# Attention without row maxima behind a branch on the chip, and the scan's C rows made on TensorE

## The chip, the core and the metric

The kernel runs on one core of a Trainium2 chip. The core has five engines with their own instruction queues: TensorE (PE in the profile, its weight loads are PEld), VectorE (DVE), ScalarE (ACT), GpSimd (POOL) and SyncE (SP, which here only issues transfers). They meet at semaphores. SBUF is the working memory of 128 partitions, PSUM takes the results of TensorE. The metric is the time of one execution in microseconds, as the device measures it; lower is better. All data are 32-bit floats.

## What is computed

Four images of 128 channels and 64x64 pixels pass four layers. Each layer is `x + f(group_norm(x))`, with 32 groups. In `f` stand, one after the other: full attention over the 4096 pixels, a 5x5 convolution, a state-space scan in two directions, and a 3x3 convolution. The two layers that the change touches are these (cut to what matters):

```python
# layer 0, n = 4096 pixels, c = 128 channels
q = einsum('bnc,dc->bnd', xt, Wq) + bq            # k and v likewise
scores = einsum('bic,bjc->bij', q, k) * c ** -0.5
attn = softmax(scores, axis=-1)
out = einsum('bij,bjc->bic', attn, v)

# layer 2, for each half of 64 channels (the second runs backwards in time)
xc = silu(causal_conv4(u)); xt = xc.transpose(0, 2, 1)
delta = softplus(xt @ Wd + bd)
Bm = xt @ WB                                       # 64 states n
Cm = xt @ WC
dA = exp(delta[..., None] * A)
dBx = (delta * xt)[..., None] * Bm[:, :, None, :]
h[t] = dA[t] * h[t-1] + dBx[t]                     # for each channel d and state n
y = einsum('bldn,bln->bld', h, Cm) + Dp * xt
```

## The kernel before

The program is written out without loops on the chip. An image lives in SBUF as 128 channels by 4096 pixels; almost every operation works on a tile of 128 partitions by 1024 columns (`CH`), of which there are four (`NCH`). A matrix product of that size is two instructions of 512 columns, and each of them appears in the profile as two matmul records and two weight loads. PSUM is given out in two pools of two buffers each: `psum_s` for short results and `psum_a` for accumulators. Work tiles come from `w2` (two buffers for each tag) and `w3` (three).

The Python program gives the tasks and the data they need; a scheduler sets the order in each engine's queue, and within a queue instructions run in that order. Each waits on semaphores for its inputs, and for the last reader of the buffer that it overwrites.

**Attention** (`attention`, line 218). After the group norm, `qT` (already scaled) and `kT` are made with channels on partitions, and `v` with pixels on partitions. Queries are taken in four blocks `qb` of 1024. For the softmax the kernel first finds the maximum of every score row: `row_max_piece` (line 245) makes a tile of scores with queries on partitions, `pmax`, on TensorE, and VectorE reduces it to a column (`part`, line 252). There are 32 such pieces for a block. `row_max_spread` (line 254) turns the 1024 maxima into a tile `mb` in which every partition holds them. The pieces of the first block run alone, ahead of the loop (line 268); those of block `qb + 1` are put between the steps of block `qb` (line 282).

The loop over the 32 key tiles `j` makes scores with keys on partitions (`sc`, TensorE), subtracts `mb` (`sm`, line 285, VectorE), takes the exponential (`pt`, line 287, ScalarE), adds it to a running sum (`lsum`, line 292, GpSimd) and multiplies it with the values (`values`, line 276, TensorE, into `acc`), one step behind the scores. At the end of a block a product with a matrix of ones (`pl`) sums `lsum` over partitions, VectorE takes the reciprocal (`rec`, line 299) and multiplies, and GpSimd adds the result to the image (line 302). In the first image the weights of the 5x5 convolution are also built on VectorE in this stretch (`build_conv_weights`).

**Scan** (`scan_layer`, line 345). A stage that I call the preparation makes `xc`, `delta` and `dx = delta * xc`, and the B and C rows of all states: two products, `pB` and `pCm`, are copied to SBUF (`bs`, `cs`) and written to DRAM (`bmat`, `cmat`). Channels of the forward half lie on partitions 0 to 63, those of the backward half on 64 to 127, and `bdiag` holds the weights of both halves on the diagonal.

Then comes the loop of four chunks `c` of 1024 time steps and 64 states `n`, 256 states for each image. For one state: four transfers on SP's queue bring the B row and the C row of each half from DRAM, repeated over its 64 partitions (`bb`, `cc`, line 427); ScalarE makes `da` (line 432); GpSimd makes `db = dx * bb` (line 434); VectorE runs the recurrence `h` (line 436, a scan along the tile) and multiplies by the C row, `hc = cc * h` (line 442); TensorE adds `hc` to `yacc` with an identity matrix as weights (`add_state`), one state behind. ScalarE keeps the last column of `h` for the next chunk (`last`, line 440). `db`, `h`, `da` and `hc` have two buffers each, so `db` of state n + 2 waits until `h` of state n has been computed. At the end of a chunk VectorE takes `yacc` over into `yn` (line 449), and after four chunks a product `po` and a sum close the layer.

These are the lines on which the order in the scan rests:

```python
db = w2.tile([P, CH], F32, tag="w1", name=f"db_{uid}")
nc.gpsimd.tensor_tensor(db, dx[:, cut], bb, ALU.mult)
h = w2.tile([P, CH], F32, tag="w2", name=f"h_{uid}")
nc.vector.tensor_tensor_scan(
    h, da, db, 0.0 if c == 0 else last[n], ALU.mult, ALU.add
)
hc = w2.tile([P, CH], F32, tag="w4", name=f"hc_{uid}")
nc.vector.tensor_tensor(hc, cc, h, ALU.mult)
```

Of the kernel before, what the change touches and what calls it, by code (L numbers as in the profile page):

```python
# [25 lines left out]
P = 128  # L26
# [3 lines left out]
MM = 512  # L30
HALF = P // 2
PAD = 2


BQ, BK, BX, BP, CONVB, BD, DSKIP, MAINB, CONVW, ALOG = 0, 1, 2, 3, 4, 5, 6, 7, 8, 12
# [3 lines left out]
def conv_preact_kernel(  # L39
# [41 lines left out]
    def psum_s(name):  # L81
        return ps_s.tile([P, CH], F32, tag="s", name=name)

    def psum_a(name):
        return ps_a.tile([P, CH], F32, tag="a", name=name)

    def matmul_ch(dst, lhsT, rhs, start=True, stop=True):
        for h in range(CH // MM):
            cut = bass.ts(h, MM)
            nc.tensor.matmul(dst[:, cut], lhsT, rhs[:, cut], start=start, stop=stop)  # L90
# [36 lines left out]
    def col(i):  # L127
        return vec[:, i : i + 1]
# [6 lines left out]
    for d in range(2):  # L135
        r = slice(d * HALF, (d + 1) * HALF)
        nc.gpsimd.tensor_copy(bdiag[r, :, r], ssm_sb[r, :, :])

    a_neg = const.tile([P, NST], F32, name="a_neg")
    nc.scalar.activation(a_neg, vec[:, ALOG : ALOG + NST], AF.Exp)  # L140
# [74 lines left out]
        nc.vector.tensor_scalar(dst, src, gm, rs, ALU.subtract, ALU.mult)  # L215


    def attention(b, xs, after_qkv):
        xn = big.tile([P, L], F32, tag="b0", name=f"xn0_{b}")
        group_norm(xs, xn, f"a{b}")  # L220
        qT = big.tile([P, L], F32, tag="b1", name=f"qT_{b}")
        kT = big.tile([P, L], F32, tag="b2", name=f"kT_{b}")
        v = big.tile([P, NJT, C], F32, tag="b4", name=f"v_{b}")
        for c in range(NCH):
            cut = bass.ts(c, CH)
            pq = psum_s(f"pq_{b}_{c}")
            matmul_ch(pq, wm[:, 0, :], xn[:, cut])
            nc.vector.tensor_scalar(qT[:, cut], pq, col(BQ), scale, ALU.add, ALU.mult)
            pk = psum_s(f"pk_{b}_{c}")
            matmul_ch(pk, wm[:, 1, :], xn[:, cut])  # L230
            nc.scalar.activation(kT[:, cut], pk, AF.Identity, bias=col(BK))
        for c in range(NCH):
            pv = psum_a(f"pv_{b}_{c}").rearrange("p (t c) -> p t c", c=C)
            for t in range(TPB):
                j = c * TPB + t
                nc.tensor.matmul(
                    pv[:, t, :], xn[:, bass.ts(j, P)], wm[:, 2, :], start=True, stop=True
                )
            bvb = bv_b.unsqueeze(1).to_broadcast([P, TPB, C])
            nc.vector.tensor_tensor(v[:, c * TPB : (c + 1) * TPB, :], pv, bvb, ALU.add)  # L240
        after_qkv()

        parts = {}

        def row_max_piece(qb, i):

            t, kc = divmod(i, NCH)
            if i == 0:
                parts[qb] = small.tile([P, TPB, NCH], F32, tag="part", name=f"part_{b}_{qb}")
            pp = psum_s(f"pmax_{b}_{qb}_{i}")  # L250
            matmul_ch(pp, qT[:, qb * CH + t * P : qb * CH + (t + 1) * P], kT[:, bass.ts(kc, CH)])
            nc.vector.tensor_reduce(parts[qb][:, t, kc : kc + 1], pp, AX.X, ALU.max)  # L252

        def row_max_spread(qb):

            m = small.tile([P, TPB], F32, tag="rmax", name=f"rmax_{b}_{qb}")
            nc.vector.tensor_reduce(m, parts.pop(qb), AX.X, ALU.max)
            pb = psum_s(f"pmb_{b}_{qb}")
            for t in range(TPB):
                nc.tensor.matmul(  # L260
                    pb[:, bass.ts(t, P)], m[:, t : t + 1].to_broadcast([P, P]), ident,
                    start=True, stop=True,
                )
            mb = w2.tile([P, CH], F32, tag="w0", name=f"mb_{b}_{qb}")
            nc.scalar.copy(mb, pb)  # L265
            return mb

        for i in range(NJT):
            row_max_piece(0, i)
        for qb in range(NCH):  # L270
            mb = row_max_spread(qb)
            acc = psum_a(f"acc_{b}_{qb}")
            lsum = w2.tile([P, CH], F32, tag="w1", name=f"lsum_{b}_{qb}")
            weights = []

            def values(j):
                matmul_ch(acc, v[:, j, :], weights[j], start=j == 0, stop=j == NJT - 1)

            for j in range(NJT):
                sc = psum_s(f"sc_{b}_{qb}_{j}")  # L280
                matmul_ch(sc, kT[:, bass.ts(j, P)], qT[:, bass.ts(qb, CH)])
                if qb + 1 < NCH:
                    row_max_piece(qb + 1, j)
                sm = w2.tile([P, CH], F32, tag="w2", name=f"sm_{b}_{qb}_{j}")
                nc.vector.tensor_tensor(sm, sc, mb, ALU.subtract)  # L285
                pt = w3.tile([P, CH], F32, tag="w3", name=f"pt_{b}_{qb}_{j}")
                nc.scalar.activation(pt, sm, AF.Exp)  # L287
                weights.append(pt)
                if j == 1:
                    nc.gpsimd.tensor_tensor(lsum, weights[0], pt, ALU.add)  # L290
                elif j > 1:
                    nc.gpsimd.tensor_tensor(lsum, lsum, pt, ALU.add)  # L292
                if j > 0:
                    values(j - 1)
            values(NJT - 1)
            pl = psum_s(f"pl_{b}_{qb}")
            matmul_ch(pl, ones, lsum)
            rec = w2.tile([P, CH], F32, tag="w2", name=f"rec_{b}_{qb}")
            nc.vector.reciprocal(rec, pl)
            nc.vector.tensor_tensor(rec, acc, rec, ALU.mult)  # L300
            cut = bass.ts(qb, CH)
            nc.gpsimd.tensor_tensor(xs[:, cut], xs[:, cut], rec, ALU.add)


    def conv(b, xs, weights, k, bias, name, finished=None):
# [39 lines left out]
    def scan_layer(b, xs):  # L345
# [25 lines left out]
        delta = big.tile([P, L], F32, tag="b3", name=f"delta_{b}")  # L371
        dx = big.tile([P, L], F32, tag="b4", name=f"dx_{b}")
        bmat = dram.tile([P, L], F32, tag="bmat", name=f"bmat_{b}")
        cmat = dram.tile([P, L], F32, tag="cmat", name=f"cmat_{b}")
        for c in range(NCH):
            cut = bass.ts(c, CH)
            pb = psum_s(f"pB_{b}_{c}")
            matmul_ch(pb, bdiag[:, 1, :], xc[:, cut])
            bs = w2.tile([P, CH], F32, tag="w0", name=f"bs_{b}_{c}")
            nc.scalar.copy(bs, pb)  # L380
            nc.sync.dma_start(bmat[:, cut], bs)
            pcm = psum_s(f"pCm_{b}_{c}")
            matmul_ch(pcm, bdiag[:, 2, :], xc[:, cut])
            cs = w2.tile([P, CH], F32, tag="w4", name=f"cs_{b}_{c}")
            nc.vector.tensor_copy(cs, pcm)
            nc.scalar.dma_start(cmat[:, cut], cs)

            pz = psum_s(f"pz_{b}_{c}")  # L390
            matmul_ch(pz, bdiag[:, 0, :], xc[:, cut])
            nc.vector.tensor_scalar(delta[:, cut], pz, col(BD), 0.0, ALU.add, ALU.max)
            e = w2.tile([P, CH], F32, tag="w1", name=f"e_{b}_{c}")
            nc.scalar.activation(e, pz, AF.Abs, bias=col(BD))
            nc.scalar.activation(e, e, AF.Exp, scale=-1.0)
            u1 = w2.tile([P, CH], F32, tag="w2", name=f"u1_{b}_{c}")
# [10 lines left out]
        c_dnt = cmat.rearrange("(d n) t -> d n t", d=2)  # L407
# [4 lines left out]
        for c in range(NCH):  # L412
# [7 lines left out]
            for n in range(NST):  # L420
                uid = f"{b}_{c}_{n}"

                bb = w3.tile([P, CH], F32, tag="w3", name=f"bb_{uid}")
                cc = w3.tile([P, CH], F32, tag="cc", name=f"cc_{uid}")
                for to, of_dnt in ((bb, b_dnt), (cc, c_dnt)):
                    for d in range(2):
                        nc.sync.dma_start(
                            to[d * HALF : (d + 1) * HALF, :],
                            of_dnt[d, n : n + 1, cut].to_broadcast([HALF, CH]),
                        )  # L430
# [11 lines left out]
                nc.vector.tensor_tensor(hc, cc, h, ALU.mult)  # L442
                held.append(hc)
                if n > 0:
                    add_state(n - 1)
# [85 lines left out]
```

## Time and profile before

| | |
|---|---|
| time, median of 3 runs | 10353.79 us (10353.5 to 10355.77) |
| profiled execution, its own time | 10353.79 us |
| profiled execution, span from first to last instruction | 10352.1 us |
| mean granted TensorE clock | 0.769 of full speed |
| PE busy | 7380.1 us (71%) |
| DVE busy | 7715.1 us (75%) |
| ACT busy | 1958.2 us (19%) |
| POOL busy | 3692.0 us (36%) |
| moved by DMA | 1113.78 MB |

The four images follow one another with hardly any overlap, so the span shows the same picture four times. The page cuts the span into 40 slices, ten for an image; a digit is the busy share in tenths, PEclk the granted clock:

```profile
PE   8998555556999855555699975555569997555556
DVE  6542999998454299999845439999975533999997
POOL 2450444443245044444224404444422441444442
PEclk9999666666999966666799986666679998666667
DMA  0000777775000077777500017777750001777774
```

Each row of ten reads from left to right: about four slices of attention and the 5x5 convolution, then about six of scan, the 3x3 convolution at their edge. A sum over the whole span mixes these stages, whose limits differ; what an operation costs has to be read in its own stage.

### The profile page before, as it was taken

The page shows a single profiled execution, that of the slowest core. Times are in us where ns is not written, and L with a number is a line of the kernel's source. Part 1 is how long each engine was busy: PE and PEld are TensorE (multiplying, and loading weights), DVE is VectorE, ACT ScalarE, POOL GpSimd, SP SyncE. Part 2 cuts the span into 40 slices and gives each one's busy share as a digit, 9 for nine tenths or more (in the row PEclk, how much of TensorE's full clock was granted, in tenths as well). Part 3 has the DMA queues.
Part 4 walks back from the last instruction along what each step waited for, and adds up shares of the span by engine and source line. Part 5 has one row for each costly group of instructions (what it writes and reads, how often), then busy time and mean ns, then how long its engine had stood idle before and what let it go on. Part 6 is the DMA issues. An engine that isn't in the chain of part 4 may idle for free. (4 is left out here: it accounts for less than half of the span.)

```text
span 10352.1 us, 46831 instructions
## 1 busy us (share of the span) xinstructions
PE 7380.1 (71%) x13504; PEld 2812.2 (27%) x13504; DVE 7715.1 (75%) x3693; ACT 1958.2 (19%) x2458; POOL 3692.0 (36%) x1618
## 2 busy tenths in 40 slices
PE   8998555556999855555699975555569997555556
PEld 3443111112444311111244431111124443111112
DVE  6542999998454299999845439999975533999997
ACT  1121222221122122222112212222111221222211
POOL 2450444443245044444224404444422441444442
PEclk9999666666999966666799986666679998666667
DMA  0000777775000077777500017777750001777774
GB/s 29 0 0 25 176 179 178 182 178 139 15 0 0 29 181 178 178 182 178 133 13 0 0 36 182 180 178 182 178 126 2 0 0 45 184 179 179 182 178 117
DMA packets 337445, 1113.78 MB, mean 108 GB/s; under 512 B 66976, under 2 KB 67616, under 8 KB 336672
## 3 DMA queue, kind: packets, MB, share of 16 engines
q1 hardware_dynamic: 334160, 1101.26, 42.3%
q10 hardware_dynamic: 3024, 9.51, 0.2%
q8 instruction: 106, 1.74, 0.1%
q14 instruction: 155, 1.27, 0.0%
HBM read 1085.34 MB, written 25.17 MB: 107 GB/s over the span
## 5 line engine op out<-in xcount | busy, mean ns | idle before, releaser
L90 PE MATMUL yacc<-hc,ident 128*128 128x512 f32 x4096 | 3414.5, 981 | 2620.4 <-DVE hc L442 2620.4
L434 POOL TENSOR_TENSOR db<-dx,bb 128x1024 f32<-128x1024 f32 x1024 | 2436.3, 2379 | 3492.0 <-DVE h L436 3489.7
L442 DVE TENSOR_TENSOR hc<-cc,h 128x1024 f32<-128x1024 f32 x1024 | 3408.8, 3329 | 93.8 <-issue 3.6
L90 PEld LDWEIGHTS yacc<-hc,ident 128*128 128x128 f32 x4096 | 1050.8, 283 | 4984.1 <-DVE hc L442 4036.7
L436 DVE TENSOR_TENSOR_SCAN h<-da,last,db 128x1024 f32<-128x1024 f32 x768 | 1846.5, 2404 | 0.4
L292 POOL TENSOR_TENSOR lsum<-lsum,pt 128x1024 f32<-128x1024 f32 x480 | 1125.8, 2345 | 1128.8 <-ACT pt L287 1128.8
L285 DVE TENSOR_TENSOR sm<-sc,mb 128x1024 f32<-128x1024 f32 x512 | 626.1, 1223 | 1083.1 <-PE sc L90 1082.9
L432 ACT ACTIVATE da<-delta,a_neg 128x1024 f32<-128x1024 f32 x1024 | 1172.7, 1145 | 1170.0 <-DVE h L436 1169.8
L90 PE MATMUL pmax<-kT,qT 128*128 128x512 f32 x2048 | 951.9, 596 | 41.6 <-DVE part L252 26.5
L90 PE MATMUL sc<-qT,kT 128*128 128x512 f32 x2048 | 964.3, 593 | 20.6 <-ACT mb L265 13.2
L90 PE MATMUL acc<-pt,v 128*128 128x512 f32 x2048 | 962.1, 592 | 3.3 <-ACT pt L287 3.3
L287 ACT ACTIVATE pt<-sm 128x1024 f32<-128x1024 f32 x512 | 541.0, 1057 | 1867.2 <-DVE sm L285 1864.5
L440 ACT COPY last<-h 128x1 f32<-128x1 f32 x768 | 146.9, 191 | 3534.3 <-DVE h L436 3534.3
L252 DVE TENSOR_REDUCE part<-pmax 128x1 f32<-128x1024 f32 x512 | 626.5, 1224 | 211.7 <-PE pmax L90 211.5
L320 PE MATMUL pce<-xpe,cw 128*128 128x512 f32 x1600 | 699.5, 599 | 13.3 <-DVE xpe L215 13.3
L436 DVE TENSOR_TENSOR_SCAN h<-da,db 128x1024 f32<-128x1024 f32 x256 | 609.0, 2379 | 19.2 <-POOL db L434 19.2
L90 PEld LDWEIGHTS pmax<-kT,qT 128*128 128x128 f32 x2048 | 387.8, 190 | 540.8 <-issue 424.4
L90 PEld LDWEIGHTS sc<-qT,kT 128*128 128x128 f32 x2048 | 387.7, 190 | 507.3 <-issue 476.8
L90 PEld LDWEIGHTS acc<-pt,v 128*128 128x128 f32 x2048 | 388.8, 190 | 494.4 <-issue 484.5
L329 DVE TENSOR_TENSOR x<-pce,x 128x1024 f32<-128x1024 f32 x16 | 19.6, 1225 | 669.3 <-PE pce L320 669.3
L320 PEld LDWEIGHTS pce<-xpe,cw 128*128 128x128 f32 x1600 | 304.0, 190 | 405.9 <-issue 392.2
L320 PE MATMUL pcm<-xpm,m 128*128 128x512 f32 x576 | 258.2, 609 | 13.3 <-DVE xpm L215 13.3
(143 smaller groups left out, 1639.6 us busy)
## 6 DMA issues: line engine op xcount, KB each, us to landing
cc<-cmat SPq DMA_DIRECT2D x2048, 256.0 KB, 4.1
bb<-bmat SPq DMA_DIRECT2D x2048, 256.0 KB, 4.9
bmat<-bs SPq DMA_DIRECT2D x16, 512.0 KB, 3.0
cmat<-cs ACTq DMA_DIRECT2D x16, 512.0 KB, 2.6
out_dram<-x SPq DMA_DIRECT2D x16, 512.0 KB, 2.6
x<-in_x_dram SPq DMA_DIRECT2D x3, 2048.0 KB, 8.2
x<-in_x_dram SPq DMA_DIRECT2D x4, 512.0 KB, 6.5
xx_sb<-in_xhat_dram SPq DMA_DIRECT2D x1, 1600.0 KB, 13.5
```

Of the source, the lines that this page charges most:

```text
L90: nc.tensor.matmul(dst[:, cut], lhsT, rhs[:, cut], start=start, stop=stop)
L252: nc.vector.tensor_reduce(parts[qb][:, t, kc : kc + 1], pp, AX.X, ALU.max)
L285: nc.vector.tensor_tensor(sm, sc, mb, ALU.subtract)
L287: nc.scalar.activation(pt, sm, AF.Exp)
L292: nc.gpsimd.tensor_tensor(lsum, lsum, pt, ALU.add)
L320: nc.tensor.matmul(acc[:, bass.ts(h, MM)].rearrange("p (r w) -> p r w", w=W), weights[:, t, :], xp[:, y : y + rows, dx : dx + W], start=t ...
L329: nc.vector.tensor_tensor(xs[:, cut], acc, xs[:, cut], ALU.add)
L432: nc.scalar.activation(da, delta[:, cut], AF.Exp, scale=a_neg[:, n : n + 1])
L434: nc.gpsimd.tensor_tensor(db, dx[:, cut], bb, ALU.mult)
L436: nc.vector.tensor_tensor_scan(h, da, db, 0.0 if c == 0 else last[n], ALU.mult, ALU.add)
L440: nc.scalar.copy(last[n], h[:, CH - 1 : CH])
L442: nc.vector.tensor_tensor(hc, cc, h, ALU.mult)
```

## The change

Three things change.

- **Attention gets a second form.** After `qT`, `kT` and `v`, the largest squared norm of the queries and of the keys is found: the tiles are squared on ScalarE, summed over channels with the matrix of ones on TensorE (`pn`), and reduced on VectorE. The product of the two bounds the square of every score. If it is at most 1600 (`SAFE_SCORE` squared), the exponentials can't overflow and no maximum need be subtracted. Every engine loads the outcome into a register and branches. One arm, `softmax_plain`, takes the exponential straight from the scores in PSUM; the other, `softmax_shifted`, is the old form. Both are in the program, one after the other.
- **The C rows are no longer stored.** `pCm`, `cs` and `cmat` go. For each state ScalarE copies the state's column of C weights, repeated 64 times for each half, into a 128x128 tile `wsel`; a product of `wsel` with `xc` gives the C row on all partitions in PSUM (`pc`, in the profile `pC`), and `hc` reads it there.
- **The B row comes in one transfer** over all 128 partitions in place of two over 64.

The old form of attention stays as it was, under a new name. The diff, cut to its core (moved lines left out):

```diff
+SAFE_SCORE = 40.0
...
+    wc_dn = bdiag[:, 2, :].rearrange("p (d n) -> p d n", d=2)
...
+    def softmax_plain(b, xs, qT, kT, v):
+
+        for qb in range(NCH):
+            cut = bass.ts(qb, CH)
+            acc = psum_a(f"facc_{b}_{qb}")
+            lsum = w2.tile([P, CH], F32, tag="w1", name=f"flsum_{b}_{qb}")
+            weights = []
+
+            def values(j):
+                matmul_ch(acc, v[:, j, :], weights[j], start=j == 0, stop=j == NJT - 1)
+
+            for j in range(NJT):
+                sc = psum_s(f"fsc_{b}_{qb}_{j}")
+                matmul_ch(sc, kT[:, bass.ts(j, P)], qT[:, cut])
+                pt = w3.tile([P, CH], F32, tag="w3", name=f"fpt_{b}_{qb}_{j}")
+                nc.scalar.activation(pt, sc, AF.Exp)
+                weights.append(pt)
+                if j == 1:
+                    nc.gpsimd.tensor_tensor(lsum, weights[0], pt, ALU.add)
+                elif j > 1:
+                    nc.gpsimd.tensor_tensor(lsum, lsum, pt, ALU.add)
+                if j > 0:
+                    values(j - 1)
+            values(NJT - 1)
+            pl = psum_s(f"fpl_{b}_{qb}")
+            matmul_ch(pl, ones, lsum)
+            rec = w2.tile([P, CH], F32, tag="w2", name=f"frec_{b}_{qb}")
+            nc.vector.reciprocal(rec, pl)
+            nc.vector.tensor_tensor(rec, acc, rec, ALU.mult)
+            nc.gpsimd.tensor_tensor(xs[:, cut], xs[:, cut], rec, ALU.add)
+
+    def softmax_shifted(b, xs, qT, kT, v):
...
+        most = small.tile([P, 2, NCH], F32, tag="most", name=f"most_{b}")
+        for i, src in enumerate((qT, kT)):
+            for c in range(NCH):
+                sq = w2.tile([P, CH], F32, tag="w2", name=f"sq_{b}_{i}_{c}")
+                nc.scalar.activation(sq, src[:, bass.ts(c, CH)], AF.Square)
+                pn = psum_s(f"pn_{b}_{i}_{c}")
+                matmul_ch(pn, ones, sq)
+                nc.vector.tensor_reduce(most[:, i, c : c + 1], pn, AX.X, ALU.max)
+        both = small.tile([P, 2], F32, tag="both", name=f"both_{b}")
+        nc.vector.tensor_reduce(both, most, AX.X, ALU.max)
+        prod = small.tile([P, 1], F32, tag="prod", name=f"prod_{b}")
+        nc.vector.tensor_tensor(prod, both[:, 0:1], both[:, 1:2], ALU.mult)
+        small_i = small.tile([P, 1], I32, tag="small_i", name=f"small_i_{b}")
+        nc.vector.tensor_scalar(small_i, prod, SAFE_SCORE * SAFE_SCORE, None, ALU.is_le)
+        is_small = nc.values_load(small_i[0:1, 0:1], min_val=0, max_val=1)
+        with tc.If(is_small > 0) as small_scores:
+            softmax_plain(b, xs, qT, kT, v)
+        with small_scores.Else():
+            softmax_shifted(b, xs, qT, kT, v)
...
-        cmat = dram.tile([P, L], F32, tag="cmat", name=f"cmat_{b}")
...
-            pcm = psum_s(f"pCm_{b}_{c}")
-            matmul_ch(pcm, bdiag[:, 2, :], xc[:, cut])
-            cs = w2.tile([P, CH], F32, tag="w4", name=f"cs_{b}_{c}")
-            nc.vector.tensor_copy(cs, pcm)
-            nc.scalar.dma_start(cmat[:, cut], cs)
...
-                cc = w3.tile([P, CH], F32, tag="cc", name=f"cc_{uid}")
-                for to, of_dnt in ((bb, b_dnt), (cc, c_dnt)):
-                    for d in range(2):
-                        nc.sync.dma_start(
-                            to[d * HALF : (d + 1) * HALF, :],
-                            of_dnt[d, n : n + 1, cut].to_broadcast([HALF, CH]),
-                        )
+                nc.sync.dma_start(bb, b_dnt[:, n : n + 1, cut].to_broadcast([2, HALF, CH]))
+                wsel = w3.tile([P, 2, HALF], F32, tag="wsel", name=f"wsel_{uid}")
+                nc.scalar.copy(wsel, wc_dn[:, :, n : n + 1].to_broadcast([P, 2, HALF]))
+                pc = psum_s(f"pC_{uid}")
+                matmul_ch(pc, wsel.rearrange("p d e -> p (d e)"), xc[:, cut])
+
...
-                nc.vector.tensor_tensor(hc, cc, h, ALU.mult)
+                nc.vector.tensor_tensor(hc, pc, h, ALU.mult)
```

More of the change, by code (lines that the diff above doesn't have):

```diff
@@ L215, in group_norm @@
         nc.vector.tensor_scalar(dst, src, gm, rs, ALU.subtract, ALU.mult)
[L218 to L237, printed above, removed]
-                )
-            bvb = bv_b.unsqueeze(1).to_broadcast([P, TPB, C])
-            nc.vector.tensor_tensor(v[:, c * TPB : (c + 1) * TPB, :], pv, bvb, ALU.add)
-        after_qkv()
@@ L302, in attention @@
             nc.gpsimd.tensor_tensor(xs[:, cut], xs[:, cut], rec, ALU.add)
+    def attention(b, xs, after_qkv):
+        xn = big.tile([P, L], F32, tag="b0", name=f"xn0_{b}")
+        group_norm(xs, xn, f"a{b}")
+        qT = big.tile([P, L], F32, tag="b1", name=f"qT_{b}")
+        kT = big.tile([P, L], F32, tag="b2", name=f"kT_{b}")
+        v = big.tile([P, NJT, C], F32, tag="b4", name=f"v_{b}")
+        for c in range(NCH):
+            cut = bass.ts(c, CH)
+            pq = psum_s(f"pq_{b}_{c}")
+            matmul_ch(pq, wm[:, 0, :], xn[:, cut])
+            nc.vector.tensor_scalar(qT[:, cut], pq, col(BQ), scale, ALU.add, ALU.mult)
+            pk = psum_s(f"pk_{b}_{c}")
+            matmul_ch(pk, wm[:, 1, :], xn[:, cut])
+            nc.scalar.activation(kT[:, cut], pk, AF.Identity, bias=col(BK))
+        for c in range(NCH):
+            pv = psum_a(f"pv_{b}_{c}").rearrange("p (t c) -> p t c", c=C)
+            for t in range(TPB):
+                j = c * TPB + t
+                nc.tensor.matmul(
+                    pv[:, t, :], xn[:, bass.ts(j, P)], wm[:, 2, :], start=True, stop=True
+                )
+            bvb = bv_b.unsqueeze(1).to_broadcast([P, TPB, C])
+            nc.vector.tensor_tensor(v[:, c * TPB : (c + 1) * TPB, :], pv, bvb, ALU.add)
+        after_qkv()
+        most = small.tile([P, 2, NCH], F32, tag="most", name=f"most_{b}")
+        for i, src in enumerate((qT, kT)):
+            for c in range(NCH):
+                sq = w2.tile([P, CH], F32, tag="w2", name=f"sq_{b}_{i}_{c}")
[14 more added lines that the diff above has]
+            softmax_shifted(b, xs, qT, kT, v)
@@ L406, in scan_layer @@
         b_dnt = bmat.rearrange("(d n) t -> d n t", d=2)
-        c_dnt = cmat.rearrange("(d n) t -> d n t", d=2)
         last = [
@@ L423, in scan_layer @@
                 bb = w3.tile([P, CH], F32, tag="w3", name=f"bb_{uid}")
-                cc = w3.tile([P, CH], F32, tag="cc", name=f"cc_{uid}")
-                for to, of_dnt in ((bb, b_dnt), (cc, c_dnt)):
-                    for d in range(2):
-                        nc.sync.dma_start(
-                            to[d * HALF : (d + 1) * HALF, :],
-                            of_dnt[d, n : n + 1, cut].to_broadcast([HALF, CH]),
-                        )
+                nc.sync.dma_start(bb, b_dnt[:, n : n + 1, cut].to_broadcast([2, HALF, CH]))
[3 more added lines that the diff above has]
+                matmul_ch(pc, wsel.rearrange("p d e -> p (d e)"), xc[:, cut])
                 da = w2.tile([P, CH], F32, tag="w0", name=f"da_{uid}")
```

## The prediction

> **What bounds the kernel now.** I read three views in this order: the table of stages, the costliest groups, then the timeline of single engines inside the two long stages. The table of stages, for the first image (attention, 5x5 convolution, preparation of the scan, scan, 3x3 convolution; columns: stretch, its length, busy time of PE, weight load, DVE, ACT and POOL, then TensorE clock, DMA share, GB/s):
>
> ```profile
> 137.50:784.00 646.50, 620.27 (x1477) 276.21 (x1476) 312.99 (x249) 139.31 (x132) 301.50 (x133) 0.99 0.00 0
> 784.00:967.00 183.00, 175.87 (x404) 76.98 (x404) 13.58 (x19) 0.00 (x0) 0.65 (x2) 0.98 0.00 0
> 967.00:1046.00 79.00, 37.59 (x64) 14.12 (x64) 58.14 (x49) 34.41 (x31) 12.01 (x9) 0.74 0.29 93
> 1046.00:2538.50 1492.50, 853.98 (x1024) 262.86 (x1024) 1456.93 (x520) 311.00 (x447) 607.15 (x256) 0.63 0.72 178
> ```
>
> Attention is bound by PE (620 of 646 us), the scan by DVE (1457 of 1492). The scan's DVE rows do not fit together, as the groups show:
>
> ```profile
> L442 DVE TENSOR_TENSOR hc<-cc,h 128x1024 f32<-128x1024 f32 x1024 | 3408.8, 3329 | 93.8 <-issue 3.6
> L285 DVE TENSOR_TENSOR sm<-sc,mb 128x1024 f32<-128x1024 f32 x512 | 626.1, 1223 | 1083.1 <-PE sc L90 1082.9
> L299 DVE RECIPROCAL rec<-pl 128x1024 f32<-128x1024 f32 x16 | 104.9, 6557 | 70.4 <-PE pl L90 70.4
> ```
>
> The same operation on the same shape takes 3329 ns as `hc` (both inputs in SBUF) and 1223 ns as `sm` (one input in PSUM). DVE and POOL side by side, first in the usual rhythm of the scan:
>
> ```profile
> 1499.03 2.34 DVE L436 TENSOR_TENSOR_SCAN h<-da,last,db 128x1024 f32<-128x1024 f32 x1
> 1501.45 2.34 POOL L434 TENSOR_TENSOR db<-dx,bb 128x1024 f32<-128x1024 f32 x1 [3.42 <-DVE h L436]
> 1501.46 3.42 DVE L442 TENSOR_TENSOR hc<-cc,h 128x1024 f32<-128x1024 f32 x1
> 1504.80 2.34 DVE L436 TENSOR_TENSOR_SCAN h<-da,last,db 128x1024 f32<-128x1024 f32 x1
> ```
>
> A scan releases the `db` after next; `db` starts 10 ns ahead of `hc`, and `hc` lasts 3.42 = 2.34 + 1.08: it stands still until `db` ends. Scans start 5.77 apart. At the start of a chunk the turns are swapped:
>
> ```profile
> 1426.56 1.23 DVE L442 TENSOR_TENSOR hc<-cc,h 128x1024 f32<-128x1024 f32 x1
> 1426.60 3.38 POOL L434 TENSOR_TENSOR db<-dx,bb 128x1024 f32<-128x1024 f32 x1 [2.23 <-DVE h L436]
> 1427.70 4.43 DVE L436 TENSOR_TENSOR_SCAN h<-da,last,db 128x1024 f32<-128x1024 f32 x1
> ```
>
> Here `hc` runs freely, `db` is held, and the scan is held by `db` in turn: it ends at 1432.13, 2.15 after `db` (1429.98). In attention the two engines overlap and neither suffers:
>
> ```profile
> 8394.00 2.35 POOL L292 TENSOR_TENSOR lsum<-lsum,pt 128x1024 f32<-128x1024 f32 x1 [1.02 <-ACT pt L287]
> 8394.98 1.22 DVE L285 TENSOR_TENSOR sm<-sc,mb 128x1024 f32<-128x1024 f32 x1 [2.21 <-PE sc L90]
> ```
>
> [...]matmul records stand 0.43 us apart in dense work and 0.86 in much of the scan, whose clock is 0.63.[...]
>
> **Unit of PE work.** A tile of 128x1024 is four matmul records, 4 x 0.429 = 1.717 us at full clock. Steady attention confirms it: `sm` stands 3.43 apart where a key tile costs scores and values (2 x 1.717), 5.15 apart where the row maxima run too (3 x 1.717).
>
> **Part 1: attention.** The reference inputs give products of the largest squared norms of 395 to 489 in the four images, against the limit of 1600, so the arm without maxima runs. Before, from the first `pmax` to the start of the last `x` addition: 44.97 to 774.83, 2652.5 to 3350.5, 5229.5 to 5925.5, 7803.2 to 8499.1, that is 730 + 698 + 696 + 696 = 2820 us.
>
> After, per image:
> - The bound: 8 tiles through `ones`, 13.7 us on PE; the squares on ACT (1.05 to 1.15 each, by the rows of `e` and `da`) and the reductions on DVE (1.22) hide beside them. Then the last reduction and three tiny DVE operations (0.16 to 0.19 each), 2.0[...]. PE, idle meanwhile, restarts slowly: 2.0. Sum 18.4. In image 1 the convolution weights share DVE: in the built order 17 operations at 1.73 and 8 reductions at 1.13 lie ahead of the branch, so 45.3 instead. All engines wait for this one value, SP too, whose queue holds only transfers needed much later.
> - Four query blocks: 32 x 2 + 1 (`pl`) = 65 tiles x 1.717 = 111.6. POOL's sum (2.35 per tile) and ACT's exponential (1.06) hide under 3.43. Between blocks `pl` and the next scores share two PSUM buffers: the second score tile waits for the reciprocal, 6.7 less one score tile 1.7 = 5.0, plus 0.7 for the last sum and 2.0 of slow clock (a 2.67 us gap before `po` cost 2.0: 16 records took 8.89 instead of 6.9). Three blocks 3 x 119.3; the last 111.6 + 0.7 + 6.6 + 1.3 = 120.2. Sum 478.1.
> - The exit: six of the eight `st_e` now stand behind the branch, 1.2 more than POOL's addition hides. [...]Sum 3.2; image 1 also finishes the weights there, 12.4.
>
> Images 2 to 4: 499.7 each; image 1: 45.3 + 478.1 + 3.2 + 12.4 = 539.0. Total 2038, a gain of 782.
>
> **Part 2: the scan.** `hc` reads `pC` from PSUM: 1.23, not held. The built order puts scan n+1 before `hc` n. A scan ends at T; POOL's `db` runs T+0.07 to T+2.42; `hc` T to T+1.22; the next scan then waits for `db` and ends 2.15 after it, T+4.57. So the stall doesn't vanish, it moves from `hc` to the scan, and the period falls from 5.77 to 4.57. What lies beside: PE has `yacc` and `pC`, 3.43 at full clock, 75% of the period; ACT has `last` 0.19, `da` 1.14 and the new `wsel`, about 0.29 (between `last` with 1 element at 0.19 and `mb` with 1024 at 1.01): 1.62; SP issues one transfer instead of four, and a `bb` has three periods less one `db`, 11.4 us, to land (median 4.9). A `pC` is needed 6.7 us after its buffer comes free. An image: 256 x 4.57 = 1170, plus chunk ends: `yn` takes 2.57 on DVE and two scans then stand without an `hc` between, which puts two `db` in a row ahead of the next; 5 each (2.9 now), 20. 1190 against 1492: gain 302, four times 1208.
>
> **Part 3: preparation.** Four `pCm` tiles and `cs` copies (1.22) go. DVE is busy 58 of 79 us there and also waits for ACT's chain; between 0 and 8 per image, taken 5: 20.
>
> **Sum.** 782 + 1208 + 20 = 2010. Profiled span 10352.1 - 2010 = 8342; launch and end lie 1.7 around the span (10353.79 for that execution, also the median): 8344 us.
>
> **Rivals.**
> - PE stays at half clock in the scan. Then four tiles take 6.87 per state, PE is the bound, and 1024 x (6.87 - 5.77) = +1126 outweighs the 802 of the other parts: 10680, slower. The turning point is 6.55 per state. For it: clock 0.63 and 0.86 spacing in this stage now. Against: at half clock PE would be busy without a break, and every stage where it is stands at 0.98 or 0.99; the late bursts at 2526 to 2536 (1.98 busy, 1.6 idle) stayed at full speed. A mix of clocks, average 5.2 to 5.6 per state, gives about 9000 to 9400.
> - `hc` is held by POOL all the same. Then the period stays near 5.6 and only 170 of the 1208 remains: 9380. Against: `sm` over `lsum` above.
> - The scan isn't held by `db` in the new order. Then DVE's 2.34 + 1.23 = 3.6 bounds: 8344 - 1024 x 0.97 = 7350. Against: the 4.43.
> - The change doesn't do what it says: the old arm runs. Gain of part 1 lost and 80 added: 9200. The inputs speak against it.
>
> **How the numbers follow.** Forecast 0.80; mixed clock 0.06; `hc` still held 0.05; scan free 0.03; old arm 0.02; half clock 0.04. The forecast's own range: 0.1 us on 1024 periods is 100, branch and block tails 60, chunk ends 60, preparation 20, so 8150 to 8600; it holds the 0.80 nearly whole, and I stretch it a little for small delays that add up: 8130 to 8680. About 0.2% is what a measurement can tell from no change. Faster 0.95, same 0.01, slower 0.04.
>
> **What would show it.** `hc<-pC,h` near 1.23; scans near 3.4 with POOL's `db` ending 2.15 before them, 4.57 apart; scan-stage clock near 1; `fpt` 3.43 apart with a gap of about 5 us of PE after each `fpl`; no `pmax`. I am wrong if scans stand at 2.34, `hc` at 3.4, or yacc records 0.86 apart.

## The result and the profile after

| | before | after |
|---|---|---|
| time, median | 10353.65 us (10350.27 to 10355.77, 4 runs) | 13803.06 us (13798.54 to 13806.13, 4 runs) |
| ratio after / before | | 1.333, 95% interval 1.331 to 1.336 |
| span of the profiled execution | 10352.1 us | 13801.2 us |
| mean granted TensorE clock | 0.769 | 0.791 |
| moved by DMA | 1113.78 MB | 568.47 MB |

The change made the kernel a third slower. The slices of the span after the change, drawn as those of the kernel before:

```profile
PE   8955555556995555555699555555569955555556
DVE  2133333333103333333310433333331043333333
POOL 4312222221431222222153222222215322222221
PEclk9977777777997777777799777777779977777777
DMA  0001111111001111111100111111110011111111
```

The two or three slices of attention and 5x5 convolution are few and dense, as they were meant to be. The other seven or eight of each image are scan, and in them no engine is busy more than about six tenths of the time. DMA, at 7 before, is at 1.

The stages of the first image after the change (attention, 5x5 convolution, preparation, scan; columns: stretch, its length, busy time of PE, weight load, DVE, ACT and POOL, TensorE clock, DMA share, GB/s):

```profile
87.00:577.00 490.00, 452.17 (x1045) 199.11 (x1046) 54.48 (x32) 130.94 (x128) 300.82 (x133) 0.96 0.00 1
577.00:785.00 208.00, 186.09 (x420) 80.43 (x419) 34.44 (x37) 2.48 (x3) 0.65 (x2) 0.94 0.00 0
785.00:827.00 42.00, 21.00 (x40) 7.81 (x40) 31.53 (x26) 29.64 (x29) 6.78 (x7) 0.87 0.16 63
827.00:3400.00 2573.00, 1477.66 (x2032) 567.33 (x2032) 892.18 (x517) 358.74 (x701) 605.84 (x258) 0.74 0.13 52
```

The scan takes 2573 us where it took 1492. DVE is busy for 892 of them where it was busy for 1457 of 1492, so the work on DVE became cheaper and something else holds it up. The last two columns say what: the DMA engines move 52 GB/s at a busy share of 0.13, against 178 GB/s at 0.72 before. A share of 0.13 of sixteen engines is as much as 2.1 engines working all the time. The packets of the transfers, each one row of 4096 bytes or a few bytes, are in the trace too: from 1000 to 3200 us there are never fewer than two in flight and hardly ever more than three, where in the scan of the kernel before (1200 to 2400 us) 14 or more are in flight for 59% of the time.

The rows of the page that answer to those shown of before, and the chain of waits (its shares by engine, then by line):

```profile
DMA 69%; PE 21%; POOL 6%; DVE 3%; issue 1%; ACT 0%; POOLq 0%; ACTq 0%; DVEq 0%; SPq 0%
...
L483 POOL TENSOR_TENSOR db<-dx,bb 128x1024 f32<-128x1024 f32 x1024 | 2397.9, 2342 | 7894.3 <-DMA bb<-bmat 7894.3
L485 DVE TENSOR_TENSOR_SCAN h<-da,last,db 128x1024 f32<-128x1024 f32 x768 | 1805.6, 2351 | 5025.4 <-POOL db L483 5025.4
...
L491 DVE TENSOR_TENSOR hc<-pC,h 128x1024 f32<-128x1024 f32 x1024 | 1227.1, 1200 | 0.8
```

`hc` fell from 3329 to 1200 ns and the scan stands at 2351 ns; neither is slowed by POOL any more. But every one of the 1024 `db` waits for its transfer, 7894.3 us in all, 7.7 each, and DMA makes up 69% of the chain. Side by side on the timeline of the scan:

```profile
2399.52 2.34 POOL L483 TENSOR_TENSOR db<-dx,bb 128x1024 f32<-128x1024 f32 x1 [7.70 <-DMA bb<-bmat]
2401.89 2.35 DVE L485 TENSOR_TENSOR_SCAN h<-da,last,db 128x1024 f32<-128x1024 f32 x1 [6.57 <-POOL db L483]
2404.16 1.20 DVE L491 TENSOR_TENSOR hc<-pC,h 128x1024 f32<-128x1024 f32 x1
...
2409.55 2.34 POOL L483 TENSOR_TENSOR db<-dx,bb 128x1024 f32<-128x1024 f32 x1 [7.69 <-DMA bb<-bmat]
```

The period is 10.03 us. The chain of waits in order of time shows one transfer from release of its buffer to landing (start, length, what):

```profile
2401.89 27.59 DMA bb<-bmat
...
2429.62 2.35 POOL db L483
```

27.6 us: with three buffers three transfers are under way, and one lands every 10.03 us. At the start of the first image's scan nothing is queued ahead. The timelines of SP (issues of the first six transfers, merged into one line; the first alone at 814.45, the second not before 829.13) and then of POOL show the time without a queue:

```profile
814.45 43.76 SPq L474 DMA_DIRECT2D bb<-bmat  x6
```

```profile
826.76 2.34 POOL L483 TENSOR_TENSOR db<-dx,bb 128x1024 f32<-128x1024 f32 x1 [9.66 <-DMA bb<-bmat]
...
841.85 2.34 POOL L483 TENSOR_TENSOR db<-dx,bb 128x1024 f32<-128x1024 f32 x1 [6.16 <-DMA bb<-bmat]
851.90 2.34 POOL L483 TENSOR_TENSOR db<-dx,bb 128x1024 f32<-128x1024 f32 x1 [7.71 <-DMA bb<-bmat]
```

The `db` of the first transfer starts 12.3 us after the issue. From the second on the `db` follow 10 us apart. A tile of `bb` is 128 x 1024 x 4 = 524288 bytes; over 10.03 us that is the 52 GB/s of the table, so 26 GB/s for each if two engines carry it. Before, a transfer of 256 KB had landed in 4.9 us (median).

Where the time went, by stages, summed over the four images from the first instruction of each stage on the timelines (attention: first `pmax` or `pn` to first `pce`; preparation: first `pB` to first scan; scan: to first `pcm`):

| stage | before | after | difference |
|---|---|---|---|
| attention | 2857.6 | 1998.9 | -858.7 |
| preparation | 215.6 | 176.7 | -38.9 |
| scan | 6051.6 | 10394.2 | +4342.6 |
| convolutions and the rest | 1227.3 | 1231.4 | +4.1 |

Attention and preparation gained; the scan lost five times as much as the two together.

### The profile page after: what moved, and what is told of

It reads as the page before. It is cut to its first block, busy times and chain, and to the rows that moved or that the text cites. A ratio compares the mean times of both kernels' runs of the same rounds, so it can differ in the third digit from the quotient of the medians.

```text
span 13801.2 us, 45087 instructions
## 1 busy us (share of the span) xinstructions
PE 9017.2 (65%) x15360; PEld 3636.0 (26%) x15360; DVE 4240.3 (31%) x2681; ACT 2139.8 (16%) x3490; POOL 3663.4 (27%) x1618
## 2 busy tenths in 40 slices
DMA packets 140581, 568.47 MB, mean 41 GB/s; under 512 B 3233, under 2 KB 3873, under 8 KB 139809
## 4 chain that ended last, share of the span: by engine, by line
DMA 69%; PE 21%; POOL 6%; DVE 3%; issue 1%; ACT 0%; POOLq 0%; ACTq 0%; DVEq 0%; SPq 0%
DMA bb<-bmat 69%; PE fsc L91 6%; PE facc L91 6%; POOL db L483 6%; PE pce L377 5%; PE pcm L377 2%; DVE xc L422 0%; PE pn L91 0%; DVE u L412 0%; POOL flsum L240 0%; PE pq L91 0%; PE fpl L91 0%; PE pk L91 0%; ACT fpt L235 0%; PE pv L332 0%
## 5 line engine op out<-in xcount | busy, mean ns | idle before, releaser
L483 POOL TENSOR_TENSOR db<-dx,bb 128x1024 f32<-128x1024 f32 x1024 | 2397.9, 2342 | 7894.3 <-DMA bb<-bmat 7894.3
L485 DVE TENSOR_TENSOR_SCAN h<-da,last,db 128x1024 f32<-128x1024 f32 x768 | 1805.6, 2351 | 5025.4 <-POOL db L483 5025.4
L91 PE MATMUL pC<-xc,wsel 128*128 128x512 f32 x4096 | 2503.7, 744 | 12.4 <-ACT e L445 12.4
L91 PEld LDWEIGHTS pC<-xc,wsel 128*128 128x128 f32 x4096 | 1159.2, 283 | 1810.8 <-issue 1793.0
L240 POOL TENSOR_TENSOR flsum<-flsum,fpt 128x1024 f32<-128x1024 f32 x480 | 1124.3, 2342 | 497.5 <-ACT fpt L235 496.5
L491 DVE TENSOR_TENSOR hc<-pC,h 128x1024 f32<-128x1024 f32 x1024 | 1227.1, 1200 | 0.8
L91 PE MATMUL fsc<-qT,kT 128*128 128x512 f32 x2048 | 965.4, 594 | 43.1 <-DVE small_i L354 29.0
L91 PE MATMUL facc<-fpt,v 128*128 128x512 f32 x2048 | 959.7, 592 | 0.0
L235 ACT ACTIVATE fpt<-fsc 128x1024 f32<-128x1024 f32 x512 | 523.8, 1023 | 1312.3 <-PE fsc L91 1304.5
L91 PEld LDWEIGHTS fsc<-qT,kT 128*128 128x128 f32 x2048 | 388.6, 190 | 539.8 <-issue 511.7
L91 PEld LDWEIGHTS facc<-fpt,v 128*128 128x128 f32 x2048 | 389.0, 190 | 489.9 <-issue 483.9
L476 ACT COPY wsel<-bdiag 128x128 f32<-128x128 f32 x1024 | 286.0, 281 | 57.9 <-PE pC L91 45.5
```

What stands on the lines that cost most here:

```text
L235: nc.scalar.activation(pt, sc, AF.Exp)
L476: nc.scalar.copy(wsel, wc_dn[:, :, n : n + 1].to_broadcast([P, 2, HALF]))
L485: nc.vector.tensor_tensor_scan(h, da, db, 0.0 if c == 0 else last[n], ALU.mult, ALU.add)
L491: nc.vector.tensor_tensor(hc, pc, h, ALU.mult)
```

## The experiments

My theory was that the form of the one transfer is the whole fault. The old code fetched `bb` by two transfers, each from one row repeated over 64 partitions. The new source has three dimensions: 2 halves, 64 repeats with stride zero, 1024 columns, the slowest being the 2. The share of 0.13 is 2.1 of sixteen engines, and two or three packets are in flight: I took the 2 of the slowest dimension for the number of engines that carry the transfer, and the runs below test this with 2, 4 and 64. The rivals: the transfers are late whatever their form (memory, or the new order in SP's queue); one transfer in flight is carried worse than two; and, once the transfers are fast, PE at half clock (`yacc` records 0.86 us apart in place of 0.43) binds.

### The row of B in two transfers again

```diff
-                nc.sync.dma_start(bb, b_dnt[:, n : n + 1, cut].to_broadcast([2, HALF, CH]))
+                for d in range(2):
+                    nc.sync.dma_start(
+                        bb[d * HALF : (d + 1) * HALF, :],
+                        b_dnt[d, n : n + 1, cut].to_broadcast([HALF, CH]),
+                    )
```

> The changed kernel with the rows of B fetched as before, in two transfers of 64 partitions each; nothing else differs. Theory (the single transfer is the only thing that failed: its source has a slowest dimension of 2 and so is carried by 2 DMA engines): the wait of db for bb goes, scans stand 4.57 us apart, the scan stage of an image falls from 2573 to about 1190 us, so 13803 - 4 x 1383 = about 8270 us. Rival A (the new queue order or the memory behind bb is late whatever the form of the transfer): about 13800 us. Rival B (PE at half clock binds the scan once the transfers are fast, 6.87 us per state): about 10500 us.

Measured: 8242.23 us, 0.796 of before (0.795 to 0.797). The undone edit alone takes 5561 us off the changed kernel. The table of stages of this run, over 800 us of the first image's scan:

```profile
1150.00:1950.00 800.00, 646.27 (x1391) 252.61 (x1390) 774.94 (x351) 242.94 (x469) 411.95 (x174) 0.99 0.41 114
```

DVE is again busy without a break (775 of 800), at 0.99 of the TensorE clock, with 114 GB/s. The rhythm in it, on the timeline of POOL and DVE:

```profile
1405.00 2.36 POOL L487 TENSOR_TENSOR db<-dx,bb 128x1024 f32<-128x1024 f32 x1 [2.23 <-DVE h L489]
...
1406.17 3.33 DVE L489 TENSOR_TENSOR_SCAN h<-da,last,db 128x1024 f32<-128x1024 f32 x1
...
1409.43 1.19 DVE L495 TENSOR_TENSOR hc<-pC,h 128x1024 f32<-128x1024 f32 x1
...
1410.76 3.33 DVE L489 TENSOR_TENSOR_SCAN h<-da,last,db 128x1024 f32<-128x1024 f32 x1
```

A `db` waits for a scan to release its buffer, and no longer for a transfer; `hc` runs freely; the scan is held until `db` ends at 1407.36 and itself ends 2.14 later, at 1409.50. Scans stand 4.59 apart here. Lateness whatever the form and PE at half clock are both out.

### The same transfer in the kernel before

```diff
-                for to, of_dnt in ((bb, b_dnt), (cc, c_dnt)):
-                    for d in range(2):
+                nc.sync.dma_start(bb, b_dnt[:, n : n + 1, cut].to_broadcast([2, HALF, CH]))
+                for d in range(2):
...
```

`cc` keeps its two transfers.

> The kernel before with one edit: the rows of B (not those of C) fetched by one transfer whose source has the slowest dimension 2. Theory (two DMA engines per transfer): db again waits for bb, a period of 10.0 us in place of 5.77, so 10354 + 1024 x 4.26 = about 14700 us. Rival A (the transfer's form is harmless, what is late in the changed kernel comes of its other edits): 10350 us, unchanged or a few us faster.

Measured: 16966.38 us, 1.639 of before (1.636 to 1.641). The edit alone ruins the kernel before as well, and by more than expected: (16966 - 10355) / 1024 is 6.5 us per state in place of 4.3, a period of 12.2. Its DMA moves 85 GB/s in the scan, half of them for `cc`, so 42 for `bb`, where the changed kernel has 52. SP's own waits (who waited for whom, us in total, times, longest) name a suspect:

```profile
SPq L427 <- DVE hc L442: 6678.4, 881, 10.4
```

The transfers of `cc` wait in SP's queue for the late `hc` to release a buffer (3395.6 us in the kernel before), and the next `bb` stands behind them. But the packets speak against this as the cause: from 1500 to 3800 us never fewer than two are in flight, so the wait in the queue leaves no gap. For 80% of the time they are two or three, the `bb` alone; for the rest up to 23, while a `cc` is under way too. An estimate from these packets: the 128 of a `bb`, 0.16 us each, keep two engines busy for 10.3 us; if the 128 of `cc`, 0.23 us each, are spread evenly over sixteen engines, eight of them add 1.8 us to each of the two, which makes 12.1 of the 12.2. By this estimate the 2.2 us are the share of `cc` that the two engines carry; the trace doesn't name the engine of a packet, so it is not shown.

### Two transfers, cut by columns

```diff
-                nc.sync.dma_start(bb, b_dnt[:, n : n + 1, cut].to_broadcast([2, HALF, CH]))
+                for s in range(2):
+                    part = bass.ds(c * CH + s * MM, MM)
+                    nc.sync.dma_start(
+                        bb[:, bass.ts(s, MM)],
+                        b_dnt[:, n : n + 1, part].to_broadcast([2, HALF, MM]),
+                    )
```

> The changed kernel with the single transfer cut into two by columns: each covers all 128 partitions and 512 columns, and each source still has the slowest dimension 2. Theory (the slowest dimension sets the number of engines[...]): period about 10.0 us, 13800 us. Rival C (one transfer in flight is carried poorly, two are enough, as before): about 8270 us. In between, a period of about 5 us, if the two transfers get different engines.

Measured: 14180.83 us, 1.369 of before (1.367 to 1.372). The table of stages over 2200 us of the scan:

```profile
1000.00:3200.00 2200.00, 1227.21 (x1688) 471.45 (x1688) 736.99 (x430) 298.22 (x598) 493.92 (x211) 0.74 0.13 51
```

51 GB/s at a share of 0.13. The number of transfers is not the point: two with a slowest dimension of 2 are as slow as one (14181 us against 13803). Two or three packets are in flight for 99.8% of this stretch, so the two halves don't run side by side on different pairs of engines. Whether both use the same pair is not shown: the trace doesn't name the engine of a packet.

### One transfer, the 64 repeats slowest

```diff
-                nc.sync.dma_start(bb, b_dnt[:, n : n + 1, cut].to_broadcast([2, HALF, CH]))
+                both_d = b_dnt[:, n : n + 1, cut].rearrange("d o t -> o d t")
+                nc.sync.dma_start(bb, both_d.to_broadcast([HALF, 2, CH]))
```

> The changed kernel with one transfer of the same bytes, whose source runs over 64 repeats as its slowest dimension and over the two directions inside it. The rows of the two directions come to lie on alternate partitions in place of the two halves, so this leaves the pairing of rows and channels out of the computation; work and sizes are the same. Theory (slowest dimension decides[...]): as e1, about 8270 us, period 4.57. Rival C (a single transfer is the fault): about 13800 us.

Measured: 8242.05 us, within 0.2 us of the version with two transfers. One transfer of the same bytes is as good as two when its slowest dimension is 64. The issues on the pages (how many, size of one, median us to landing), first of this run, then of the run with two transfers:

```profile
bb<-bmat SPq DMA_DIRECT2D x1024, 512.0 KB, 3.8
bb<-bmat SPq DMA_DIRECT2D x2048, 256.0 KB, 3.9
```

The single transfer lands in 3.8 us, each of the two in 3.9. Merging two transfers into one was thus neither harmful nor useful by itself: SP's issues, halved from 2048 to 1024, were not the limit.

### One transfer, slowest dimension 4

```diff
-        b_dnt = bmat.rearrange("(d n) t -> d n t", d=2)
+        b_qmt = bmat.rearrange("(q m) t -> q m t", q=4)
...
-                nc.sync.dma_start(bb, b_dnt[:, n : n + 1, cut].to_broadcast([2, HALF, CH]))
+                m = n % (HALF // 2)
+                nc.sync.dma_start(bb, b_qmt[:, m : m + 1, cut].to_broadcast([4, HALF // 2, CH]))
```

> The changed kernel with one transfer of the same bytes, whose source has the slowest dimension 4 (four row blocks, each repeated 32 times). Which row goes to which channel differs, so this leaves the pairing of rows and channels out of the computation; work and sizes are the same. Theory (the slowest dimension is the number of engines that carry a transfer): half the landing time of 2 engines, so 10.03 / 2 = 5.0 us per state, a little above the 4.58 that the scan needs itself: 8242 + 1024 x 0.45 = about 8700 us. Rival (only 2 is bad, 4 is spread like 64): 8242 us. Rival (any such pattern that isn't a plain repeat is as slow as 2): 13800 us.

Measured: 8677.49 us, 0.838 of before (0.837 to 0.839). The table of stages over 800 us of the scan, and POOL's timeline in it:

```profile
1100.00:1900.00 800.00, 594.67 (x1272) 231.87 (x1270) 556.36 (x323) 224.61 (x454) 383.58 (x159) 0.99 0.26 104
```
```profile
1400.91 2.36 POOL L484 TENSOR_TENSOR db<-dx,bb 128x1024 f32<-128x1024 f32 x1 [2.66 <-DMA bb<-bmat]
1405.93 2.35 POOL L484 TENSOR_TENSOR db<-dx,bb 128x1024 f32<-128x1024 f32 x1 [2.66 <-DMA bb<-bmat]
```

Twice the share (0.26), twice the rate (104 GB/s), half the period (5.02). With 2, 4 and 64 as slowest dimension the transfer is worth 10.03 us, 5.02 us and nothing that shows. A second sign of the number of engines needs no rate. In this run four or five packets are in flight for 99.5% of the stretch, where the changed kernel has two or three and the dimension 64 reaches 14 and more. And the pages count small packets, here of the changed kernel, of this one, and of the one with 64:

```profile
DMA packets 140581, 568.47 MB, mean 41 GB/s; under 512 B 3233, under 2 KB 3873, under 8 KB 139809
DMA packets 142628, 568.48 MB, mean 66 GB/s; under 512 B 5280, under 2 KB 5920, under 8 KB 141856
DMA packets 154916, 568.53 MB, mean 69 GB/s; under 512 B 17568, under 2 KB 18208, under 8 KB 154144
```

The bytes moved are the same, but there are 2047 and 14335 more packets under 512 bytes than in the changed kernel, two and fourteen for each of the 1024 transfers. In the traces of the scan a `bb` comes with 2, 4 and 16 packets of 4 bytes beside its 128 rows. For 2 and 4 that is also what the shares give (0.13 and 0.26 of sixteen engines are 2.1 and 4.2). The cause is settled; dimensions between 4 and 64 were not tried.

### The new attention with the old scan

The scan layer of the kernel before, put into the changed kernel in place of its own; its core:

```diff
-                nc.scalar.copy(wsel, wc_dn[:, :, n : n + 1].to_broadcast([P, 2, HALF]))
-                pc = psum_s(f"pC_{uid}")
-                matmul_ch(pc, wsel.rearrange("p d e -> p (d e)"), xc[:, cut])
+                for to, of_dnt in ((bb, b_dnt), (cc, c_dnt)):
+                    for d in range(2):
...
-                nc.vector.tensor_tensor(hc, pc, h, ALU.mult)
+                nc.vector.tensor_tensor(hc, cc, h, ALU.mult)
```

> The changed kernel's attention (bound, branch and the arm without maxima) with the scan layer of the kernel before, C rows and all four transfers per state included. The prediction gave the attention 782 us: 9574 us. Read from the trace of the run with two transfers, an image goes from the first tile of the bound to the last x addition in 477.5 us (505 in image 1) where the kernel before needs 696 to 698 (730), less about 15 us for the conv weights left behind the branch: about 860 us gained, 9490 us. What remains to 8242 is then the scan's and the preparation's part: 1250 against the predicted 1228. Rival (the parts aren't additive, one hides the other): outside 9450 to 9600 us.

Measured: 9499.21 us, 0.917 of before (0.916 to 0.919). Attention alone is worth 857 us, and the 1257 that are left to 8242 belong to scan and preparation. In the stages of the trace with two transfers attention gains 859 us, scan and preparation 1258 (1211 and 47): measured in these two ways the parts add up.

### Without bound and branch

```diff
-        most = small.tile([P, 2, NCH], F32, tag="most", name=f"most_{b}")
...
-        with tc.If(is_small > 0) as small_scores:
-            softmax_plain(b, xs, qT, kT, v)
-        with small_scores.Else():
-            softmax_shifted(b, xs, qT, kT, v)
+        softmax_plain(b, xs, qT, kT, v)
```

> The two-transfer version with the arm without maxima called outright: the bound on the scores and the branch are left out of the computation. This prices them. Theory from the trace: 16.6 us from the first tile of the bound to the first scores in images 2 to 4, 42 us in image 1, where the conv weights share VectorE, and about 15 us in image 1 for the weights that wait behind the branch: 8242 - 50 - 57 = about 8135 us. Rival (the branch costs much more than the trace's idle time shows[...]): below 8100 us. Rival (most of it is hidden): above 8200 us.

Measured: 8126.48 us, so bound and branch cost 116 us of 8242, close to the 107 read from the trace. The branch has no large price beyond the idle time that the trace shows.

### `da` in PSUM

The last experiment tests the other reading that the prediction rests on, that the scan is held (3.33 us) because it reads two operands from SBUF beside GpSimd. It starts from the version with two transfers.

```diff
-    ps_a = ctx.enter_context(tc.tile_pool(name="ps_a", bufs=2, space=PSUM))
+    ps_a = ctx.enter_context(tc.tile_pool(name="ps_a", bufs=1, space=PSUM))
...
-    def psum_a(name):
-        return ps_a.tile([P, CH], F32, tag="a", name=name)
+    def psum_a(name, turn=0):
+        return ps_a.tile([P, CH], F32, tag="ab"[turn % 2], name=name)
...
-                da = w2.tile([P, CH], F32, tag="w0", name=f"da_{uid}")
+                da = psum_a(f"da_{uid}", 1)
```

`turn` is `qb` or `c` in the attention and the convolutions.

> The two-transfer version with da written to PSUM, so that the scan reads one operand from SBUF in place of two; da has one PSUM buffer, taken from the second accumulator, which the conv and the attention still use in turns. Theory (the scan stands at 3.33 us because it reads two SBUF operands while GpSimd computes db): the scan falls to about 2.34 us beside a running db, the next da (ready 1.5 us after a scan's end) sets the period, about 3.9 us, and the kernel takes 8242 - 1024 x 0.68 = about 7550 us. Rival D (any VectorE instruction that reads db's or da's pair is slowed by GpSimd, or the scan waits for db as data): the scan stays near 3.3 and the period near 4.6, 8250 us. Rival E (PE, 3.43 us per state, drops to half clock or is late with pC): period 5 or more, over 8700 us.

Measured: 7296.26 us, 0.705 of before (0.703 to 0.706), faster than all others. The timeline of POOL and DVE:

```profile
1401.79 2.36 POOL L487 TENSOR_TENSOR db<-dx,bb 128x1024 f32<-128x1024 f32 x1 [1.33 <-DVE h L489]
...
1401.82 1.23 DVE L495 TENSOR_TENSOR hc<-pC,h 128x1024 f32<-128x1024 f32 x1
...
1403.06 2.35 DVE L489 TENSOR_TENSOR_SCAN h<-da,last,db 128x1024 f32<-128x1024 f32 x1
...
1406.75 2.35 DVE L489 TENSOR_TENSOR_SCAN h<-da,last,db 128x1024 f32<-128x1024 f32 x1
```

The scan starts at 1403.06, while a `db` is running (until 1404.15), and takes 2.35 us in place of 3.33. Scans stand 3.70 apart; I had expected 3.9, since `da` was to be the last to come, but it takes 1.11 and is ready before `hc` ends. PE is now busy for 595 of 600 us in this stage by its records, and DVE for 581.

## Why the prediction was wrong

It failed at one step of part 2: "SP issues one transfer instead of four, and a `bb` has three periods less one `db`, 11.4 us, to land (median 4.9)." The 4.9 is the landing time of the kernel before, of 256 KB with 64 as slowest dimension, in a scan with 14 or more packets in flight for 59% of the time (issues on the page: how many, size of one, median us to landing):

```profile
bb<-bmat SPq DMA_DIRECT2D x2048, 256.0 KB, 4.9
```

I carried it over to a transfer of 512 KB with 2 as slowest dimension, which keeps 0.13 of the sixteen engines busy. This one needs 12.3 us from its issue to its `db` without a queue, more than the 11.4 even then, and in a stream one comes each 10.03 us, more than twice the 4.57 at which the scan would have asked for them. I counted instructions and waits of the transfer and never its engines, although the change of `[HALF, CH]` into `[2, HALF, CH]` stands in the diff. No rival named a transfer, so the range had no room for it: 1024 x (10.03 - 4.57) = 5591 us is what the step cost, and 8344 + 5591 = 13935 comes within 1% of the 13803 measured.

Of the signs that were to show an error two did appear in the changed kernel, scans at 2.35 us and many `yacc` records 0.85 apart, but both as effects of the late `db`. The other steps, as measured in the run with two transfers, which differs from the changed kernel in the transfer alone:

| step of the prediction | predicted | measured |
|---|---|---|
| whole kernel | 8344 us | 8242 us |
| part 1, gain of attention | 782 | 859 |
| bound, images 2 to 4 / image 1 | 18.4 / 45.3 | 16.6 / 41.8 |
| four query blocks | 478.1 | 460.9 (463.0 in image 1) |
| exit, images 2 to 4 / image 1 | 3.2 / 15.6 | 2.6 / 15.9 |
| part 2, gain of the scan | 1208 | 1211 |
| period of the scan | 4.57 | 4.58 |
| part 3, gain of the preparation | 20 | 47 |

Of the 18.4 for the bound, 17.7 are terms with figures from the trace of before, and of the 3.2 for the exit 1.2; the rest, for the register load and the jump, was my estimate, which no trace of before shows.

- **Part 1** was right in kind: the plain arm ran, and all four images show it. The query blocks are the term that was too dear. I had the second score tile of a block wait for the reciprocal, 5.0 us. The timeline of the run with two transfers at the end of the first block shows that it doesn't:

```profile
200.01 1.98 PE L91 MATMUL fpl<-flsum,ones 128*128 128x512 f32 x4 [0.22 <-POOL flsum L240]
201.84 1.88 PE L91 MATMUL fsc<-qT,kT 128*128 128x512 f32 x4
202.13 6.56 DVE L247 RECIPROCAL frec<-fpl 128x1024 f32<-128x1024 f32 x1 [113.78 <-PE fpl L91]
203.81 1.02 ACT L235 ACTIVATE fpt<-fsc 128x1024 f32<-128x1024 f32 x1 [6.33 <-PE fsc L91]
204.89 1.55 PE L91 MATMUL fsc<-qT,kT 128*128 128x512 f32 x3 [1.17 <-ACT fpt L235]
```

  The second `fsc` starts at 204.89, after a wait of 1.17 us for the exponential of the first, while the reciprocal still reads `fpl` until 208.69. It took over the buffer of the first score tile and not that of `fpl`: the two buffers are not given out strictly in turn. The 2.0 us for a slow clock after the gap didn't come either: from the second record on, those of PE stand 0.43 us apart again. Blocks follow 113.5 us apart in place of 119.3, which is 70 us over four images and three block ends. The 45.3 for the bound in image 1 doesn't follow from the terms given: 17 x 1.73 + 8 x 1.13 and 4.7 at the end make 43.2, nearer to the 41.8 measured.
- **Part 2**, the transfer apart, came true to the step: `hc` at 1.19 is not held, the scan is held by `db` and ends 2.14 after it, `wsel` takes 281 ns (0.29 estimated), PE runs at 0.99 of its clock. In the changed kernel itself neither the hold nor the clock could show: `db` comes so late that scan and `db` never overlap (2351 ns), and PE, busy for 1478 of 2573 us, is granted 0.74.
- **The reason for the hold** stands firmer than before. With both operands in SBUF the scan takes 3.33 us beside a running `db`; with one of them moved to PSUM it is free (2.35).
- **Part 3** was 27 us too low. In image 1 the time from the first `pB` to the first scan fell from 54.2 to 41.8 us, more than the 8 that I had as upper end; which of the removed operations gave it I didn't separate. The changed kernel keeps 39 us of it.

## What to carry to other kernels

When a change alters the shape of a transfer, ask how many DMA engines carry the new one before asking how many transfers there are: a broadcast whose outermost dimension is 2 ran at 52 GB/s here, and the same bytes with 64 outermost, or in two transfers with 64 outermost each, were hidden entirely. A landing time read from a profile belongs to one access pattern, and not to the queue or the size: the same 512 KB on the same queue landed in 3.8 us or took 12.3. And a low DMA share in a stage that waits for DMA is the sign to look for: 0.13 was 2.1 engines of sixteen here, with two or three packets in flight without a break, and not a transfer system at rest. The packets in flight, and the small packets for each transfer, agree with the share on the number of engines: two or three and 2 at 0.13, four or five and 4 at 0.26.

## What was not expected of the hardware

- The slowest dimensions 2 and 4 gave 52 and 104 GB/s at shares of 0.13 and 0.26 (2.1 and 4.2 of sixteen engines): an estimate of 26 GB/s for each of two or four engines, with no loss between. Halving the pieces from 1024 to 512 columns cost little (14181 against 13803 us).
- An operand moved from SBUF to PSUM made a 2.35 us instruction out of one of 3.33, with nothing else in the scan changed but the number of buffers: `da` and `yacc` have one each. That single move was worth 946 us (8242 to 7296), more than the whole rebuilt attention (857).
- The branch was cheap: from the end of the comparison to the first scores PE lost 0.7 us in images 2 to 4 of the changed kernel (the register loads took 0.27 to 0.33 us there, 0.44 to 0.46 on SP, and up to 0.55 in image 1), and the exits cost 2.6 us more than those of the kernel before, the statistics for the next group norm (`st_e`) that the branch holds back included.
